# Row weighting of a graph attention layer: the order of its instructions written out over three blocks

## The chip, the core and the metric

The kernel runs on one core of a Trainium2 chip. Five engines of that core matter here, each with a queue of its own that runs in program order: TensorE (PE in the profile, with its weight loads as PEld), VectorE (DVE), ScalarE (ACT), GpSimd (POOL) and SyncE (SP), which only issues transfers. ACT, POOL and SP can all issue DMA transfers. The metric is the device time of one execution in microseconds, the median of several runs.

## What is computed

The reference takes 4096 node rows of 256 numbers and a 0/1 adjacency of 4096 x 4096, and runs two layers on them. The change touches the beginning of layer 0, a graph attention layer with 4 heads of 64:

```
h = relu(layernorm(x))
hW = (h @ W).reshape(n, 4, 64)
src = hW . a[:64];  dst = hW . a[64:]
e = leaky_relu(src[:, None] + dst[None, :], 0.2), masked by adj > 0
out = softmax(e) @ hW                 # per head
x = x + layernorm(out) * gamma + beta
```

Layer 1, a top-p diffusion over the same rows with two steps, takes most of the time and isn't changed.

## The kernel before, in words

The exponential of a leaky ReLU of a sum falls apart into products: where src + dst is positive the weight is exp(src) exp(dst), else exp(0.2 src) exp(0.2 dst). So the kernel first weights the rows: for each block b of 128 rows (32 blocks) it makes hW, multiplies each head's 64 columns by exp(dst) and by exp(0.2 dst), and appends the two factors as a 65th column. These 2 x 4 x 65 = 520 numbers (`uv`) are split into three bf16 parts, so that the later bf16 matmuls keep fp32's precision. That is the **row weighting** (lines 193 to 240). Then follow 16 **passes** (4 groups of 1024 destination rows by 4 heads). A pass walks over 16 pairs of blocks; for each pair it makes a sign matrix g (is src + dst positive?, 2 chunks of 128x1024), two masks m from g and the adjacency `ax` (lines 305 and 306), and 32 matmuls of the masks with the weighted rows `ut` (line 325).

The row weighting of one block, with its engine and line:

- DVE: statistics of the row (lines 153, 154); for each group of four blocks, POOL makes scale and bias in four small steps (lines 145 to 148).
- ACT: `hb`, the normalized row with ReLU (213). PE: two transpositions (216). ACT: the copy `hT` (218). PE: two matmuls with `wx`, the weights with eight more columns for src and dst (221). An fp32 matmul shows as two records.
- DVE: `sd_c`, src and dst of the block (222). ACT: two small exponentials (226). DVE: two products (228), which read PSUM.
- ACT: the first part, a cast (232). DVE: the first subtraction (233). ACT: the second part (237). DVE: the second subtraction, which is the third part (238).
- POOL: the copy of head 0's parts to `ut0` in SBUF (239). ACT's queue: the store of the other heads' parts to `uv_d` in DRAM (240). POOL: a small memset of the ones column (231).
- After blocks 3 and 7 (`b % 4 == 3`, below 8): four transpositions that spread src over 1024 columns into `sr0` for the first pass (245, 246). After every sixth block POOL issues a load of adjacency, `ax`, 512 KB (line 179, called at 236), so five of the eight loads start in this stage.

Before the loop, `wx` gets its eight columns by four products and sums on DVE (199, 201). After it come the transposition of src for all heads and its store `s_d` (248 to 251), the merged key weights `wkq` for layer 1 (254 to 263), d_big and d_neg (264, 265), which the signs need, and the factors `e_c` (268, 269), which the first pass needs at its end.

Buffers: three `uv` and four `st` slots (`split_rows`, `b % 4`). In this stage the program gives the operations block after block, and the framework's scheduler chooses the order in each engine's queue. The passes are different: there `manual_schedule` keeps the order in which the code calls the stages, `sign_stage(n + 3)`, `mask_stage(n + 2)`, `products(n)`, for ACT, DVE, PE and POOL. SP's order stays with the scheduler. Before the first products the signs of pairs 0 to 2 (ACT, line 299; pairs 3 and 11 of a pass are compared on DVE, line 297) and the masks of pairs 0 and 1 are made. `mask_stage` also issues, on SP, the loads of the next pass's source row `sr` (line 282, from s_d) and of its quarters `ut` (287, from uv_d), and the store of ut0's quarters (413).

Of the kernel before, what the change touches and what calls it, by code (L numbers as in the profile page):

```python
# [17 lines left out]
U8 = mybir.dt.uint8  # L18
# [38 lines left out]
def gat_then_top_p_diffusion(  # L57
# [53 lines left out]
    ln_g_r = row_vector(ln_g, "ln_g_r")  # L111
    ln_b_r = row_vector(ln_b, "ln_b_r")


    wkq = const.tile([P, KC, 2 * DA], F32, name="wkq")
    nc.scalar.dma_start(wkq[:, :, :DA], w3_t.rearrange("(k p) m -> p k m", p=P))
# [49 lines left out]
    with tc.tile_pool(name="l0", bufs=1) as l0, tc.tile_pool(name="l0s", bufs=2) as l0s, tc.tile_pool(name="l0o", bufs=1) as l0o:  # L166
        passing = ctx.enter_context(ExitStack())
        l0a, l0u = (passing.enter_context(tc.tile_pool(name=x, bufs=n)) for x, n in (("l0a", 9), ("l0u", 6)))
        gamma_r = row_vector(gamma, "gamma_r", l0)
        beta_r = row_vector(beta, "beta_r", l0)  # L170
# [17 lines left out]
        ut0 = [quarter() for q in range(4)]  # L188
        split_rows = l0o.tile([P, 4, 2 * H * (W3 + 1) // 2], F32, name="st")
        sr0 = l0s.tile([P, G0 * P], F32, name="sr")  # L190
        with tc.tile_pool(name="l0r", bufs=3) as rows, tc.tile_pool(name="l0w", bufs=1) as l0w, \
                tc.tile_pool(name="ps2", bufs=2, space=PSUM) as ps2:
            a_r = row_vector(a, "a_r", l0w)
            wx = l0w.tile([P, KC, D + 2 * H], F32, name="wx")
            nc.sync.dma_start(wx[:, :, :D], w.rearrange("(k p) m -> p k m", p=P))
            for k in range(KC):
                for i in range(2):
                    pr = rp.tile([P, H, HD], F32, name="pr", tag="hl", bufs=5)
                    nc.vector.tensor_mul(pr, wx[:, k, :D].rearrange("p (h d) -> p h d", h=H),
                                         a_r[:, None, ts(i, HD)].to_broadcast([P, H, HD]))  # L200
                    nc.vector.reduce_sum(wx[:, k, ds(D + i * H, H)], pr, axis=AX.X)
            for g in range(NB // 4):
                nc.sync.dma_start(X[:, ts(g, 4), :], x[ts(g, 4 * P), :].rearrange("(b p) d -> p b d", p=P))
            for g in range(NB // 4):
                x4 = X[:, ts(g, 4), :]
                mv = rows.tile([P, 4, nc.vector.BN_AGGR_DIM], F32, name="mv4")
                for i in range(4):
                    moments_of(mv[:, i, :], x4[:, i, :])
                rs, nmr = steps(mv, 4, rows)
                for i in range(4):  # L210
                    b = 4 * g + i
                    hb = rows.tile([P, D], F32, name="hb")
                    nc.scalar.activation(hb, x4[:, i, :], AF.Relu, scale=rs[:, i:i + 1], bias=nmr[:, i:i + 1])
                    pt = ps2.tile([P, KC, P], F32, name="tp")
                    for k in range(KC):
                        nc.tensor.transpose(pt[:, k, :], hb[:, ts(k, P)], ident)
                    hT = rp.tile([P, KC, P], F32, name="hT", tag="ar", bufs=4)
                    nc.scalar.copy(hT, pt)
                    pm = ps2.tile([P, 512], F32, name="mm", bufs=3)
                    for k in range(KC):  # L220
                        nc.tensor.matmul(pm[:, :D + 2 * H], hT[:, k, :], wx[:, k, :], start=(k == 0), stop=(k == KC - 1))
                    nc.vector.tensor_scalar(sd_c[:, :, :, b], pm[:, ds(D, 2 * H)].rearrange("p (t h) -> p t h", t=2),
                                            TINY, -TINY, ALU.add, ALU.add)
                    uv = rows.tile([P, H, 2, W1], F32, name="uv")
                    for t, scale in enumerate((1.0, ALPHA)):
                        nc.scalar.activation(uv[:, :, t, HD:], pm[:, ds(D + H, H)][:, :, None], AF.Exp, scale=scale)
                    for t in range(2):
                        nc.vector.tensor_mul(uv[:, :, t, :HD], pm[:, :D].rearrange("p (h d) -> p h d", h=H),
                                             uv[:, :, t, HD:].to_broadcast([P, H, HD]))
                    parts = split_rows[:, b % 4, :].bitcast(BF16).rearrange("p (h t w) -> p h t w", h=H, t=2)  # L230
                    set1 = nc.gpsimd.memset(parts[:, :, :, W3:], 1.0)
                    nc.scalar.copy(parts[:, :, :, :W1], uv)
                    nc.vector.tensor_tensor(uv, uv, parts[:, :, :, :W1], ALU.subtract)
                    if b % 6 == 5:
                        with tc.issue_after(set1.ins):
                            ax.append(edges(0, len(ax)))
                    nc.scalar.copy(parts[:, :, :, ds(W1, W1)], uv)
                    nc.vector.tensor_tensor(parts[:, :, :, ds(2 * W1, W1)], uv, parts[:, :, :, ds(W1, W1)], ALU.subtract)
                    nc.gpsimd.tensor_copy(ut0[b // QUARTER][:, b % QUARTER], parts[:, 0])
                    nc.scalar.dma_start(uv_d[1:, :, b].rearrange("h p t w -> p h t w"), parts[:, 1:])  # L240
                    if b % 4 == 3 and b < G0:
# [1055 lines left out]
```

## Time and profile before

| | us |
|---|---|
| median of 3 runs | 2957.44 (2957.43 to 2959.31) |
| the profiled execution | 2960.24 |
| its span, first to last instruction | 2958.3 |
| row weighting: block 0's exponential to block 31's | 22.75 to 120.80 |
| first product of the first pass | 131.3, without a gap from 131.98 |
| mean granted TensorE clock over the span | 0.987 |

Mean duration and count in the stage, from the groups of the first 155 us:

| line, engine | what | count | mean ns |
|---|---|---|---|
| 213 ACT | hb | 32 | 606 |
| 218 ACT | hT | 32 | 374 |
| 232, 237 ACT | casts 128x520 | 32 each | 636, 626 |
| 226 ACT | exponentials | 64 | 171 |
| 228 DVE | products 128x256 | 64 | 415 |
| 233, 238 DVE | subtractions 128x520 | 32 each | 724, 699 |
| 153, 154 DVE | statistics | 32 each | 400, 168 |
| 221 PE | matmuls | 128 | 518 |
| 239 POOL | copy to ut0, 128x392 bf16 | 32 | 708 |
| 146 POOL | power, one of four steps | 8 | 1102 |
| 179 POOL | adjacency issue | 8 | 840 |

How to read it: durations of neighbours on one engine overlap by about 0.1 us, so what a queue can carry is better read from start to start. An instruction that waited for a semaphore shows it as idle time before it, with the releaser; one that was held up while running shows a longer duration. Times of one engine are summed over the stage, and a full stage shows an engine near its length.

### The profile page before, as it was taken

How to read it: one execution, taken by the hardware profiler on the slowest of the kernel's cores; microseconds unless marked ns; L12 is line 12 of the kernel's file. 1: busy time of each engine (PE TensorE's matmuls, PEld its weight loads, DVE VectorE, ACT ScalarE, POOL GpSimd, SP SyncE). 2: the span in 40 equal slices, each digit the busy share in tenths (PEclk: the TensorE clock that was granted, in tenths of full speed). 3: DMA queues.
4: the chain of work that ended last, by engine and by line, in shares of the span. 5: the costliest groups of instructions: out<-in, count | busy, mean ns of one | idle time of the engine just before them, and what ended most of it. 6: DMA issues, size and time to landing. Idle time of an engine off the chain costs nothing. (4 is left out here: it accounts for less than half of the span.)

```text
span 2958.3 us, 51979 instructions
## 1 busy us (share of the span) xinstructions
PE 2829.7 (96%) x19033; PEld 2473.5 (84%) x19033; DVE 2196.5 (74%) x5195; ACT 1915.5 (65%) x3067; POOL 726.4 (25%) x1637
## 2 busy tenths in 40 slices
PE   4699999999999999999999999899999999999998
PEld 3499999999987778888888888788778888888886
DVE  6666877868754383788888888453837999999995
ACT  5768687867833544777777777234427777777772
POOL 3201111112010030322223322000203444444441
PEclk8799999999999999999999999999999999999999
DMA  6858668595454686000000000388980000001000
GB/s 154 176 208 238 187 223 194 223 235 169 191 192 156 219 277 214 19 20 20 20 20 26 20 20 18 131 272 271 330 289 22 25 25 25 25 27 31 25 23 21
DMA packets 181152, 368.16 MB, mean 124 GB/s; under 512 B 17168, under 2 KB 133904, under 8 KB 176784
## 3 DMA queue, kind: packets, MB, share of 16 engines
q1 hardware_dynamic: 129824, 261.55, 26.2%
q0 software_dynamic: 21504, 83.89, 11.9%
q10 hardware_dynamic: 29552, 19.22, 2.1%
q8 instruction: 155, 2.54, 0.3%
q14 instruction: 117, 0.96, 0.1%
HBM read 301.35 MB, written 109.38 MB: 139 GB/s over the span
## 5 line engine op out<-in xcount | busy, mean ns | idle before, releaser
L943 PE MATMUL acc<-X,eT 128*128 128x256 f32 x4096 | 968.1, 381 | 0.0
L943 PEld LDWEIGHTS acc<-X,eT 128*128 128x128 f32 x4096 | 744.8, 191 | 97.8 <-ACT eT L937 14.5
L325 PE MATMUL acc<-ut,m 128*128 128x195 bf16 (+1 forms) x8192 | 700.9, 247 | 13.9 <-DVE m L305 8.0
L325 PEld LDWEIGHTS <-m 128*128 128x128 fp8e4 x8192 | 696.6, 97 | 18.1 <-issue 9.9
L762 ACT ACTIVATE e<-mm,nm 128x1024 f32<-128x1024 f32 x256 | 286.7, 1120 | 311.6 <-PE mm L602 297.1
L299 ACT ACTIVATE g<-sr,d_big 128x1024 uint8<-128x1024 f32 x448 | 471.3, 1139 | 5.5 <-DMA s_d<-sT 2.9
L937 ACT COPY eT<-tp 128x512 f32<-128x512 f32 x512 | 299.2, 584 | 107.2 <-PE tp L935 106.3
L830 DVE SCALAR_TENSOR_TENSOR big<-e,c 128x4096 f32<-128x4096 f32 x58 | 273.0, 4707 | 121.2 <-POOL c L815 84.2
L502 PE MATMUL mm<-ar,hl 128*128 128x512 f32 x844 | 336.6, 402 | 13.1 <-DMA ar<-adj_d 5.4
L848 DVE MAX8 cand<-big 128x8 f32<-128x228 f32 (+1 forms) x1152 | 348.4, 380 | 0.0
L786 POOL TENSOR_TENSOR sums<-sums 128x2 f32<-128x2 f32 x64 | 12.5, 196 | 1313.0 <-ACT void L769 1313.0
L502 PE MATMUL acc<-ar,hl 128*128 128x512 f32 x844 | 329.4, 393 | 1.4 <-DVE ar L489 1.4
L935 PE MATMUL tp<-ident,e 128*128 128x128 f32 x2048 | 311.5, 275 | 7.8 <-DVEq L1234 5.8
L935 PEld LDWEIGHTS tp<-ident,e 128*128 128x128 f32 x2048 | 249.3, 141 | 77.2 <-ACT eT L957 27.8
L305 DVE TENSOR_TENSOR m<-g,ax 128x512 uint32<-128x512 uint32 x256 | 181.4, 709 | 127.6 <-PE acc L325 104.2
L872 DVE SCALAR_TENSOR_TENSOR e<-e,found 128x4096 f32<-128x4096 f32 x58 | 259.6, 4476 | 0.0
L769 ACT ACTIVATE void<-e,c1x 128x2048 int8<-128x2048 f32 x128 | 257.5, 2011 | 3.1 <-issue 2.2
L769 ACT ACTIVATE void<-e,c 128x2048 int8<-128x2048 f32 x128 | 257.4, 2011 | 0.0
L502 PEld LDWEIGHTS mm<-ar,hl 128*128 128x128 f32 x844 | 159.6, 189 | 52.0 <-issue 9.4
L602 PE MATMUL mm<-kT,qT 128*128 128x512 f32 x512 | 198.1, 468 | 3.6 <-ACT e L762 2.2
L306 DVE TENSOR_TENSOR m<-m,ax 128x512 uint32<-128x512 uint32 x256 | 177.1, 692 | 25.3
L502 PEld LDWEIGHTS acc<-ar,hl 128*128 128x128 f32 x844 | 159.6, 189 | 33.7 <-DVE ar L489 1.8
(262 smaller groups left out, 3444.2 us busy)
## 6 DMA issues: line engine op xcount, KB each, us to landing
ar<-adj_d SPq DMA_DIRECT2D x211, 512.0 KB, 4.6
adj_d<-ax POOLq DMA_DIRECT2D x32, 2048.0 KB, 7.0
ut<-uv_d SPq DMA_DIRECT2D x60, 784.0 KB, 5.2
aru<-adj_d SPq DMA_DIRECT2D x45, 512.0 KB, 4.5
ax<-in_adj_t_dram POOLq DMA_DIRECT2D x32, 512.0 KB, 15.7
x<-xf_d SPq DMA_DIRECT2D x78, 128.0 KB, 4.9
uv_d<-st ACTq DMA_DIRECT2D x32, 294.0 KB, 4.3
xf<-xft_d SPq DMA_DIRECT2D x64, 128.0 KB, 2.2
```

Source lines behind the costliest of these rows:

```text
L299: nc.scalar.activation(g[:, c, :], shared[k].sr, AF.Relu, scale=BIG, bias=d_big[:, h, j:j + 1])
L325: nc.tensor.matmul(shared[k].acc[i][:, t, :cols], m[t][:, c, ts(i, P)], shared[k].ut[j // QUARTER][:, j % QUARTER, t, :cols], start=(j == ...
L502: nc.tensor.matmul(A.acc[c][s], A.hl[m][:, t, ts(s, P)], A.ar[m][:, ts(c, 512)], start=(j == 0 and t == 0), stop=(j == NB - 1 and t == 1))
L602: nc.tensor.matmul(pm[:, h, :], q[t], kT[:, ds(h * (N // 2) + c * 512, 512)], start=(t == 0), stop=(t == 1))
L762: nc.scalar.activation(ev[:, :, c, :], r.pm[c], AF.Exp, bias=r.nm, accum_out=r.sums[:, c // 2, c % 2:c % 2 + 1])
L769: nc.scalar.activation(void, r.e[:, ts(h, N // 2)], (AF.Relu, AF.Sign)[i], bias=r.c1, scale=-1.0, accum_out=r.sums[:, h, 2 + i:3 + i])
L830: nc.vector.scalar_tensor_tensor(big, r.e, r.c3, r.e, ALU.is_le, ALU.mult, accum_out=r.low3)
L848: nc.vector.max(cand[:, s, :], big[:, edges[s]:edges[s + 1]])
L872: nc.vector.scalar_tensor_tensor(r.e, r.e, r.t, r.e, ALU.is_ge, ALU.mult, accum_out=kept)
L935: nc.tensor.transpose(pt[:, i, :], r.e[:, ts(4 * g + i, P)], ident)
L937: nc.scalar.copy(eT, pt)
L943: nc.tensor.matmul(r.acc[:, 0, :], eT[:, i, :], cur[:, j, :], start=(j == 0), stop=(j == NB - 1))
```

## The change

The row weighting is ordered by hand, as the passes are. The functions below are called once per block by `turn_of(b)`, which works on three blocks at once: block b is multiplied and read, block b - 1 weighed and its first part made, b - 2 gets its second part, b - 3 its third part, copy and store; block b + 1 is opened (hb and transpositions), and the statistics run six blocks ahead.

- **Loads.** The rows X are issued first on SP (group 0, then the vector a, then groups 1 to 7). wx and the small weights go by ACT's queue. gamma, beta, ln_g and ln_b come after the rows. SP's order is kept in this part.
- **Splits on GpSimd.** The second subtraction is halved: heads 0 and 1 on DVE, heads 2 and 3 on POOL. The store to uv_d is issued by SP. The memset of the ones is done once for each slot, at the start. d_big and d_neg are made on POOL, by quarters of eight blocks.
- **Buffers.** Eight slots: four of `st`, four in two free `ut` buffers. Five `uv`: three in the tile of output rows, one in the second `sr` buffer, one in an `ax` buffer. PSUM: the eight banks of the passes' accumulators serve the stage too (two for transpositions, three for products, others for spread and keys), and no pool is closed between.
- **Into the stage.** The signs of pairs 0 and 1 are made chunk by chunk on POOL in turns 14, 15, 19 and 20; the masks of these pairs in turns 30 and 31. The merged keys are made in turn 12. Six adjacency loads (blocks 1, 6, 11, 16, 21, 26) start in place of five.
- **Into the first pass.** `turn_of(32)` to `turn_of(34)`, that is the remaining splits of blocks 29 to 31, run after the products of pairs 1 to 3; the factors e_c after those of pairs 4 and 5.

The core of the diff:

```diff
-        with tc.tile_pool(name="l0r", bufs=3) as rows, tc.tile_pool(name="l0w", bufs=1) as l0w, \
-                tc.tile_pool(name="ps2", bufs=2, space=PSUM) as ps2:
...
-                    nc.scalar.copy(parts[:, :, :, :W1], uv)
-                    nc.vector.tensor_tensor(uv, uv, parts[:, :, :, :W1], ALU.subtract)
...
-                    nc.scalar.copy(parts[:, :, :, ds(W1, W1)], uv)
-                    nc.vector.tensor_tensor(parts[:, :, :, ds(2 * W1, W1)], uv, parts[:, :, :, ds(W1, W1)], ALU.subtract)
-                    nc.gpsimd.tensor_copy(ut0[b // QUARTER][:, b % QUARTER], parts[:, 0])
-                    nc.scalar.dma_start(uv_d[1:, :, b].rearrange("h p t w -> p h t w"), parts[:, 1:])
...
+            block_rows(0)
+            nc.scalar.dma_start(wx[:, :, :D], w.rearrange("(k p) m -> p k m", p=P))
+            nc.sync.dma_start(a_r, bass.AP(tensor=a.tensor, offset=a.offset, ap=[[0, P], [1, 2 * HD]]))
+            for g in range(1, NB // 4):
+                block_rows(g)
...
+            slots = [l0o.tile([P, 4, HALF], F32, name="st")] + [l0u.tile([P, 2, HALF], F32, name="slots", tag="ut") for i in range(2)]
...
+            def first_part(b):
+                nc.scalar.copy(slots[b % len(slots)][:, :, :, :W1], uvs[b % len(uvs)])
+
+            def second_part(b):
+                uv, parts = uvs[b % len(uvs)], slots[b % len(slots)]
+                nc.vector.tensor_tensor(uv, uv, parts[:, :, :, :W1], ALU.subtract)
+                nc.scalar.copy(parts[:, :, :, ds(W1, W1)], uv)
+
+            def third_part(b):
+                uv, parts = uvs[b % len(uvs)], slots[b % len(slots)]
+                for engine, h in ((nc.vector, slice(0, H // 2)), (nc.gpsimd, slice(H // 2, H))):
+                    engine.tensor_tensor(parts[:, h, :, ds(2 * W1, W1)], uv[:, h], parts[:, h, :, ds(W1, W1)], ALU.subtract)
+                seen = nc.gpsimd.tensor_copy(ut0[b // QUARTER][:, b % QUARTER], parts[:, 0])
+                nc.sync.dma_start(uv_d[1:, :, b].rearrange("h p t w -> p h t w"), parts[:, 1:])
+                if b % 5 == 1 and len(ax) < 6:
+                    with tc.issue_after(seen.ins):
+                        ax.append(edges(0, len(ax)))
...
+            def turn_of(b):
+
+                if b < NB:
+                    multiplied(b)
+                if 0 < b < NB:
+                    weighed(b - 1)
+                opened(b + 1)
+                if b % 4 == 0 and 0 < b <= G0:
+                    spread(b - 1)
+                if 0 < b <= NB:
+                    first_part(b - 1)
+                if 1 < b <= NB + 1:
+                    second_part(b - 2)
+                if 2 < b <= NB + 2:
+                    third_part(b - 3)
+                measured(b + 6)
+                if b < NB:
+                    read(b)
+                if b % QUARTER == 0 and 0 < b < NB:
+                    signed(b // QUARTER - 1)
+                if b == 12:
+                    merged_keys()
+                for n, at in enumerate((14, 19)):
+                    if at <= b < at + 2:
+                        sign_stage(n, b - at)
+                if NB - 2 <= b < NB:
+                    mask_stage(b - NB + 2)
...
-            for n in range(3):
-                sign_stage(n)
-            mask_stage(0)
-            mask_stage(1)
...
+        rest = {n: lambda b=NB - 1 + n: turn_of(b) for n in (1, 2, 3)}
+        rest.update({4 + i: lambda i=i: factors(i) for i in range(2)})
+        with tc.manual_schedule(engines=every):
+            for b in range(4):
+                measured(b)
...
+            opened(0)
+            for b in range(NB):
+                turn_of(b)
+            weighed(NB - 1)
...
+            signed(3)
+            sign_stage(2)
             for n, (k, p) in enumerate(todo):
                 if n > 0 and p == 0:
                     later.extend(evacuate(k - 1))
                 sign_stage(n + 3)
                 mask_stage(n + 2)
                 products(k, p, ms.pop(n))
+                if n in rest:
+                    rest[n]()
```

## The prediction

> **What bounds the kernel now.** I read the page's shares first, then stretches of the start by engine, then waits and groups of the first 155 us, and at last the timeline from 0 to 170 us, row by row. The shares of the span:
> ```profile
> PE 2829.7 (96%) x19033; PEld 2473.5 (84%) x19033; DVE 2196.5 (74%) x5195; ACT 1915.5 (65%) x3067; POOL 726.4 (25%) x1637
> ```
> TensorE is busy 96% of 2958.3 us, so only a place where it idles can give much. The stretches (from:to, length, busy us and instructions of PE, PEld, DVE, ACT, POOL, then granted clock, DMA share, GB/s) show the place:
> ```profile
> 20.00:40.00 20.00, 15.56 (x56) 10.85 (x54) 15.64 (x52) 13.81 (x42) 8.01 (x18) 0.91 0.39 86
> 53.27:60.28 7.01, 3.74 (x16) 2.22 (x14) 6.56 (x15) 4.86 (x15) 1.42 (x2) 1.00 1.04 102
> 80.00:100.00 20.00, 9.77 (x24) 5.57 (x23) 11.49 (x27) 10.93 (x30) 10.33 (x23) 0.59 0.60 153
> 120.00:131.30 11.30, 2.58 (x10) 1.37 (x8) 5.37 (x14) 6.86 (x15) 2.32 (x4) 0.50 0.99 163
> 131.30:175.00 43.70, 43.34 (x491) 42.88 (x492) 26.35 (x39) 32.70 (x33) 4.04 (x6) 0.96 0.74 163
> ```
> From 131.3 us TensorE is full, 43.34 of 43.70; before, in the row weighting, no engine is. From 80 to 100 us the fullest, DVE, has 11.49 of 20. So that stage is a chain of waits, and a microsecond taken from it shifts all that follows. Its waits (total us, times, longest):
> ```profile
> PEld mm L221 <- ACT hT L218: 38.5, 25, 4.9
> POOL st L231 <- DMA uv_d<-st: 32.2, 11, 8.9
> ...
> ACT hb L213 <- POOL nmr L148: 16.5, 1, 16.5
> ...
> ACT st L232 <- DMA uv_d<-st: 7.9, 4, 3.5
> ```
> The stores of the parts hold the chain: the four `st` slots are refilled only when the store of uv_d has landed (4.3 us in the middle, 11.4 at most). ACT, stopped there by program order, lets TensorE wait for `hT`. Three moments of the timeline (start, duration) divide the stage:
> ```profile
> 22.75 0.24 ACT L226 ACTIVATE uv<-mm 128x4 f32<-128x4 f32 x2 [1.16 <-DVE sd_c L222]
> ...
> 120.80 0.24 ACT L226 ACTIVATE uv<-mm 128x4 f32<-128x4 f32 x2 [0.35 <-DVE sd_c L222]
> ...
> 131.98 0.34 PE L325 MATMUL acc<-ut,m 128*128 128x196 bf16 x1 [0.36 <-DVE m L306]
> ```
> The first is block 0's exponential, the second block 31's, the third the point from which products run without a gap. So: head 22.75, middle 98.05 (31 steps of 3.16), tail 11.18.
>
> **Head.** The rows X leave first instead of at 6.15 us, behind five small loads and wx; wx goes by ACT's queue. Now a row load lands 7.0 to 9.6 us after its issue (8.6 in the middle), the first load of an empty SP queue after 3.7. Rows issued at 0.75 arrive between 0.75 + 3.7 + 1.5 (0.5 MB at the 350 GB/s of that time) = 6 and 0.75 + 8.6 = 9.4; I take 6, since the queue is empty. Then four blocks of statistics 1.6, the four GpSimd steps 1.9 (16.61 to 18.45), and from `hb` to the exponential 4.3 (18.49 to 22.75): 13.8, say 14, at worst 17.2. The wx branch is no later: 0.77 + its present 7.4, then 2.7 for the four products and sums (11.86 to 14.51), 10.9, while the first matmul comes near 12. **Gain 8.75.** The row vectors for the ends of both layers are moved behind the rows; nothing reads them for 100 us.
>
> **Middle.** Per block, from the groups:
> ```profile
> L239 POOL COPY ut<-st 128x392 bf16<-128x392 bf16 x32 | 22.5, 708 | 30.9 <-DVE st L238 30.9
> L238 DVE TENSOR_TENSOR st<-uv,st 128x520 bf16<-128x520 f32 x32 | 22.4, 699 | 2.7 <-ACT st L237 1.5 <-POOL ut L239 0.7
> ```
> ACT has hT, hb, two casts and two exponentials. Start to start in rows without a wait they take 0.26, 0.51, 0.53, 0.52 and 0.12, together 1.94; its store issue goes to SP's queue. DVE has the two products 0.67, the first subtraction 0.62, half the second 0.35, statistics 0.39, sd_c 0.1: 2.1. PE has 1.16 + 0.5 warm. The chain through a turn is exponentials 0.24, products 0.74, first cast 0.53, second 0.52 with its subtraction beside it, small hand-overs: 2.2. Five `uv` and eight slots in place of three and four let three blocks overlap; a slot is wanted again 5.5 turns after its store, 13 us, above the longest landing of 11.4. So the DMA waits go, and what is late next is this ACT/DVE chain. The present order already goes that fast where nothing stalls: 2.34 per block from 53.27 to 60.28, with the DMA at 1.04, and 2.19 for six blocks from 101.20 to 114.33. **I take 2.4**, bounds 2.19 and 2.7: 31 x 2.4 = 74.4 for 98.05, gain 23.7.
>
> GpSimd decides whether 2.4 holds. Its half of the second subtraction, 128x260, isn't in the trace; the nearest row on that engine:
> ```profile
> L376 POOL TENSOR_TENSOR X<-X,beta_r x32: 715/736/1019, 331.0 to 861.2; 128x256 f32<-128x256 f32 x32
> ```
> So 0.74, at most 1.02; below, 0.35 (DVE's rate for half). With the copy to `ut` 0.50 (1.06 at most), steps 0.48 (15.3 us for eight groups over 32 blocks) and adjacency issue 0.17, GpSimd has 1.9 per turn: it fits. It collides with DVE, though. At 56.12 a copy of 0.51 began on POOL, at 56.16 a subtraction on DVE, which took 1.02 and not 0.67. In the new order the GpSimd half runs beside DVE's products, which read PSUM and show no such stretch (407 to 421 ns), and the copy beside the statistics; hence little is lost. If nothing fits beside, DVE's 0.70 + 0.37 and GpSimd's 1.9 add to 2.96 per turn, my first rival. [...]
>
> **Put into the middle**: two `spread` copies, 1.1 of transposes or 0.6 of ACT each, 2.4 with hand-overs (they are in the 98.05 too); `merged_keys`, 2.0 by its rows at 121 to 123.9; one mask pair on DVE, 2 x 0.69 = 1.4 (the second lies behind the last exponential). Four sign chunks on GpSimd, 128x1024 each: no row. By the copy's rate (0.50 for 392) 1.3 each, by the subtraction's (0.74 for 256) 2.9; I take 1.5, since a compare reads one input as the copy does: 6 us, of which two turns of buffers hide all but 2.2. From below nothing, from above 8. [...] Sum 8.0, bounds 5 and 14.
>
> **Tail.** Now: last split to 125.3, s_d stored at 121.6, row read back at 128.28, signs, first mask at 130.5. After: signs and masks of pairs 0 and 1 lie in the middle, the last three blocks' rest beside the first products, which need only quarter 0. One transposition and its wait remain: 1.0 (0 to 2). Gain 10.2. What it adds to the first pass: ACT 1.6 for splits and 0.6 for factors against its slack, 28 signs of 1.04 in 43 us; DVE under 5 us. Two covers are thin. `uvs` takes the second `sr` buffer, so the source row of pass 1 waits for pass 0's last sign; today the next row is issued at 157.52, when TensorE is at pair 9.4 of 2.71 us, six pairs ahead. After, ACT ends near T+30 and the row lands 4.9 later, T+35, before pair 16 at T+43. Uncovered it costs up to 5 once. And uv_d's stores share SP's queue with reloads that wait for TensorE; they come earlier in the program.
>
> **Sum.** 14 + 74.4 + 8.0 + 1.0 = 97.4 for 131.98: 34.6 less. The profiled execution took 2960.24 (span 2958.3 and 1.9 around it), 2.8 above the median of the runs, 2957.44. So 2925.6 profiled, **2923** as median.
>
> **Rivals.**
> - *Turn about 2.95.* [...] 14 + 91.5 + 8 + 1 = 114.5, gain 17.5: 2940. A DMA that can't keep up ends here too: its share adds to 95 us by 131.3, and a sixth adjacency load (34 us for five) adds 6.8; but the stores need only 31 of it.
> - *Given back in the first pass.* The pass-1 row, a reload or an adjacency block comes late, TensorE idles 5 to 25: 2940 with the middle as forecast, 2950 with both.
> - *Slower.* GpSimd becomes the bound of every turn. It decides from (131.98 - 14 - 8 - 1) / 31 = 3.52 per turn, that is from 2.36 for the half subtraction in place of 0.74. With bf16 operands at three times the row, 2.2, the copy always blocked at 1.06, steps 0.7, issue 0.17 and signs at 2.9 (0.4 per turn), it is 4.5: 14 + 140 + 8 + 1 = 163, 31 later: 2988. Against it: no two-input row of 256 on POOL exceeds 1.02.
> - *It doesn't do what it says.* Landings grow with eight stores in flight and the slots still wait: the turn stays at 3.16, gain 11: 2946.
>
> **How the numbers follow.** Likeliest, turn 2.19 to 2.7: 0.62, from 12.5 + 67.9 + 5 + 1 = 86.4 (2912) to 17.2 + 83.7 + 10 + 2 = 112.9 (2938). Turn 2.95: 0.17. Given back: 0.06. Slots still wait: 0.04. Slower: 0.09. No change, by parts of these that cancel: 0.02. The range reaches below to ACT's own 1.94 per block (12.5 + 60.1 + 5 + 1 = 78.6, 2904; I stop at 2907) and above to the slots' 2946: 2907 to 2946. Faster by over 0.2% (5.9 us, about what a measurement of this kernel can tell): 0.62 + 0.17 + 0.06 + 0.04 = 0.89, less 0.01 for the ends; within 0.03; slower 0.09.
>
> **What would show it.** In the new profile: block 0's exponential near 14; exponentials 2.4 apart; no wait of ACT or POOL for uv_d; a clock near 1.0 from 20 to 95; the half subtraction on POOL near 0.74; the first products without a gap near 97, and no gap at pair 16, some 43 us later; the rest of the page the same. It is wrong if POOL has the longest busy time of the stage, if L213's successor waits for POOL's steps, or if TensorE idles after its first product.

## The result, and the profile after

| | before | after |
| --- | --- | --- |
| median of the runs, us | 2958.38 (2957.43 to 2960.55, 4 runs) | 2938.49 (2936.8 to 2939.0, 4 runs) |
| profiled execution, us | 2960.24, span 2958.3 | 2939.0, span 2937.2 |
| block 0's exponential | 22.75 | 14.46 |
| block 31's exponential | 120.80 | 114.63 |
| first product without a gap | 131.98 | 114.81 |
| head, middle, tail | 22.75, 98.05, 11.18 | 14.46, 100.17, 0.18 |

The ratio of the times is 0.9931, with a 95% interval from 0.9914 to 0.9948: 19.9 us faster, where 34.6 were forecast. The whole kernel after the change still has TensorE as its bound, as the first part of its page shows:

```profile
PE 2832.3 (96%) x19033; PEld 2476.5 (84%) x19033; DVE 2197.3 (75%) x5193; ACT 1912.0 (65%) x3063; POOL 761.9 (26%) x1657
```

Against before POOL's sum has grown by 35.5 us, PE's and PEld's by 3.0 at most. The three moments of the timeline after (start, duration, engine and line) divide the stage as before; L249 is the exponential now, L378 the product:

```profile
14.46 0.24 ACT L249 ACTIVATE o<-b 128x4 f32<-128x4 f32 x2 [1.92 <-DVE sd_c L246]
...
114.63 0.23 ACT L249 ACTIVATE o<-b 128x4 f32<-128x4 f32 x2
114.81 10.43 PE L378 MATMUL acc<-ut,m 128*128 128x196 bf16 x104
```

The head came 8.3 earlier and the tail is gone: the products start 0.18 after the last exponential, 11 less than before. The middle, which was to shrink from 98 to 82.4, is 2.1 **longer** than before. So the time to look for is 17.8 us (100.17 - 82.4), all of it between 14 and 115 us. The stretches of after (from:to, length, then busy us and instructions of PE, PEld, DVE, ACT, POOL, then granted clock, DMA share, GB/s):

```profile
40.00:60.00 20.00, 14.77 (x40) 10.06 (x41) 14.22 (x40) 14.39 (x41) 11.52 (x21) 0.57 0.69 142
60.00:80.00 20.00, 13.16 (x38) 8.35 (x37) 15.76 (x44) 13.29 (x37) 19.33 (x22) 0.66 0.65 137
80.00:100.00 20.00, 12.99 (x34) 7.97 (x33) 14.20 (x38) 11.87 (x34) 18.05 (x23) 0.57 0.77 130
...
111.00:155.00 44.00, 41.62 (x461) 40.86 (x462) 33.73 (x55) 35.59 (x43) 12.01 (x16) 0.96 0.91 212
```

Two things stand out: the granted clock is near 0.6 from 40 to 100 us, and POOL is full from 60 to 100 us (19.33 and 18.05 of 20). From 111 on TensorE is full, beside the remainders too. The waits from 0 to 115 us (total us, times, longest) name no store of uv_d any more. Another wait has grown, that of the exponential for sd_c. Before, from 0 to 132 us, it was

```profile
ACT uv L226 <- DVE sd_c L222: 7.7, 10, 1.3
```

and after it is 13.9 in 21 times, by the tile that is written:

```profile
PEld b L242 <- ACT hT L239: 39.5, 32, 2.5
...
ACT hb L232 <- POOL nmr L143: 14.6, 3, 8.3
...
ACT o L249 <- DVE sd_c L246: 10.8, 15, 1.9
...
ACT sr L249 <- DVE sd_c L246: 1.7, 3, 0.9
...
ACT uv L249 <- DVE sd_c L246: 1.4, 3, 0.6
```

The distance from one block's exponential to the next (31 of them) has its median at 3.0 us, not 2.4. Five are long: 3.95 and 5.62 (the two `spread` turns), 5.12 (the keys), 4.14 and 6.25 (the signs), together 25.1. The other 26 take 75.1, that is 2.89 each. So, counted in this way, 15.1 of the 17.8 are 31 turns of 2.89 in place of 2.4, and 2.7 are what the put-in work cost above its 8.0 (100.17 - 31 x 2.89 = 10.7). After the first product the profiled executions differ by up to 8 us (from it to the end of the span 2820 to 2828 us over before, after and the kernels below, with 2826.3 before and 2822.4 after; nothing in that part of the program differs among most of them). Nearly all of this lies in layer 1: the 16 passes take 704.7 to 707.2 in all these traces, the rest 2114 to 2122, in the main the longer the lower the granted clock there (0.997 where it is 2114.3, in e7; 0.992 where it is 2122.2, in e1). For causes in the row weighting the first product's time is therefore the cleaner measure; differences between medians below some 4 us are not read. The first product has a scatter of its own, which the end of the experiments measures.

### The profile page after: what moved, and what is told of

Its sections match the earlier page's. It is cut to its first block, busy times and chain, and to the rows that moved or that the text cites. A ratio compares the mean times of both kernels' runs of the same rounds, so it can differ in the third digit from the quotient of the medians.

```text
span 2937.2 us, 51997 instructions
## 1 busy us (share of the span) xinstructions
PE 2832.3 (96%) x19033; PEld 2476.5 (84%) x19033; DVE 2197.3 (75%) x5193; ACT 1912.0 (65%) x3063; POOL 761.9 (26%) x1657
## 5 line engine op out<-in xcount | busy, mean ns | idle before, releaser
L378 PE MATMUL acc<-ut,m 128*128 128x195 bf16 (+1 forms) x8192 | 700.5, 247 | 5.5 <-DVE st L395 5.5
L378 PEld LDWEIGHTS <-m 128*128 128x128 fp8e4 x8192 | 696.7, 97 | 9.4 <-DVE st L395 4.6
```

The source lines that it names most:

```text
L378: nc.tensor.matmul(shared[k].acc[i][:, t, :cols], m[t][:, c, ts(i, P)], shared[k].ut[j // QUARTER][:, j % QUARTER, t, :cols], start=(j == ...
```

## What ends a turn

Three theories were tried, and the change's parts were undone one by one.

- **A, cold TensorE** ("cold" is half clock, a granted clock of 0.50 in the turn at 32.06 of after, where a block's four matmuls take 2.13; "warm" is full clock, 1.00 from 53.27 to 60.28 of before, where they take 1.16). Cold, the loop matmuls, sd_c, exponential, hT, matmuls gives 3.0. The clock is the cause, and a filled TensorE cures it.
- **S, signs.** The four compares on GpSimd hold up its steps (mean and scale of later groups) and DVE.
- **C, the order at the PSUM bank.** Found on the way, in the second experiment. sd_c (DVE, L246) and the exponential (ACT, L249) both read the products' bank, and the framework orders these two readers as the program has them: the exponential waits for sd_c, 13.9 in after. sd_c stands at the end of DVE's turn, so the loop is exponential, products, subtraction, half subtraction, statistics, sd_c, exponential, on one engine and back, at any clock.

A cold turn in the timeline of after:

```profile
32.06 0.24 ACT L249 ACTIVATE o<-b 128x4 f32<-128x4 f32 x2 [0.62 <-DVE sd_c L246]
...
32.21 0.37 ACT L239 COPY hT<-b 128x256 f32<-128x256 f32 x1
32.40 0.76 DVE L254 TENSOR_TENSOR o<-b,o 128x256 f32<-128x256 f32 x2 [0.44 <-ACT o L249]
...
32.64 2.13 PE L242 MATMUL b<-wx,hT 128*128 128x264 f32 x4 [0.46 <-ACT hT L239]
33.07 0.69 DVE L262 TENSOR_TENSOR o<-o,slots 128x520 f32<-128x520 f32 x1
...
34.80 0.17 DVE L246 TENSOR_SCALAR sd_c<-b 128x8 f32<-128x8 f32 x1
35.01 0.24 ACT L249 ACTIVATE o<-b 128x4 f32<-128x4 f32 x2 [0.58 <-DVE sd_c L246]
```

Here the matmuls take 2.13 and end when sd_c can start; hT comes behind the exponential in ACT's program order, and the next matmuls behind hT. From 32.06 to 35.01 it is 2.95, and this goes round. GpSimd's work end to end with DVE's, the ground of the rival "turn about 2.95", is not what makes this turn: L262 has its 0.69 here. Over the stage DVE's subtractions are stretched in some turns. Of the 30 subtractions L262 from 18 to 114 us 22 took 0.68 to 0.69, and the eight longer ones add 2.8; of the half subtractions on DVE all but five took 0.42 or 0.43, and these five (0.73 to 0.89, most beside POOL's own half) add 2.2. That is 5 us in all, 0.16 per turn.

## The experiments

Each kernel is the changed one with the edit shown; five rounds each, against the kernel before on the same chip (that had 2953.9 to 2960.5 from chip to chip, so gains are compared, not times).

**e1: the signs on DVE.**

```diff
                 if len(only) == 1:
-                    nc.gpsimd.tensor_scalar(g[:, c, :], shared[k].sr, d_neg[:, h, j:j + 1], 255.0, ALU.is_gt, ALU.mult)
+                    nc.vector.tensor_scalar(g[:, c, :], shared[k].sr, d_neg[:, h, j:j + 1], 255.0, ALU.is_gt, ALU.mult)
```

> The four early sign chunks (pairs 0 and 1) are compared on DVE and not on GpSimd. Theory A (TensorE at the half clock sets the turn of 3.0 us, and GpSimd's compares of 3.7 us add delays in turns 15 to 23): the delays above 3.0 in turns 15, 16, 19, 22 and 23 (0.4 + 0.2 + 1.1 + 0.3 + 3.3 = 5.4 us) go, the four compares on DVE cost 0.75 each of which some shows, the other turns stay near 3.0; first product at 109 to 111 instead of 114.8, about 2933 us. [...] If the compares are hidden: 2938 to 2941.

Measured: 0.9934 [0.9921, 0.9947], gain 17.9; first product 108.6, 6.2 earlier than after's. Most turns are 2.7 to 3.0 as before, the two long sign turns are gone (none above 3.41 from turn 13 on). S holds, but not for all of the 6.2: 2.0 of them lie in turns 1 to 14, before the first sign, where the two programs are the same, and some 4.3 in turns 15 to 31. The median doesn't show them. Its cause in the trace of after is the duration itself:

```profile
L348 POOL TENSOR_SCALAR g<-sr,d_neg 128x1024 uint8<-128x1024 f32 x4 | 15.2, 3796 | 0.2
```

and what it delays, in the timeline of after:

```profile
61.31 3.72 POOL L348 TENSOR_SCALAR g<-sr,d_neg 128x1024 uint8<-128x1024 f32 x1
61.55 1.42 DVE L262 TENSOR_TENSOR sr<-sr,slots 128x520 f32<-128x520 f32 x1
```

```profile
83.99 3.70 POOL L348 TENSOR_SCALAR g<-sr,d_neg 128x1024 uint8<-128x1024 f32 x1
...
91.16 0.20 POOL L143 TENSOR_TENSOR nmr<-nmr,rs 128x4 f32<-128x4 f32 x1
91.39 0.60 ACT L232 ACTIVATE hb<-X,nmr,rs 128x256 f32<-128x256 f32 x1 [4.20 <-POOL nmr L143]
```

Signs of 3.7 put back POOL's steps for later blocks, and `hb` waits 4.20 for them. The DVE subtraction that starts 0.24 after the first sign takes 1.42 in place of 0.69 (more on this in the last section).

**e2: TensorE kept busy.** Two bf16 matmuls of 128x512 per turn, into a free bank; their result is not used.

```diff
                 opened(b + 1)
+                if b < NB:
+                    fill = in_bank(2, [P, 512])
+                    ones_ = ident.bitcast(BF16)
+                    for i in range(2):
+                        nc.tensor.matmul(fill.rearrange("p (a b) -> p a b", a=2), ones_[:, :P], ones_[:, None, :].to_broadcast([P, 2, 2 * P]), start=True, stop=True)
```

> Two matmuls without use (bf16, 128x128 by 128x512, into a PSUM bank that nothing reads) after the transpositions of each turn; all else as in the changed kernel. Theory A: they fill TensorE's wait for hT, its clock stays near 1.0, the four matmuls of a block take 1.16 and not 2.13, and the turns of 3.0 become 2.3 to 2.5; some 20 turns by 0.6 is 12 us: first product near 103, about 2926. [...] If the added work only delays TensorE: up to 0.9 us per cold turn more, 2955.

Measured: 0.9946 [0.9933, 0.996], gain 16.3; first product 112.4. The clock over the middle rises from 0.71 to 0.91 (below, the whole middle of after, then of e2), yet the middle falls by 2.6 only:

```profile
14.46:114.63 100.17, 66.21 (x200) 43.52 (x200) 74.26 (x205) 68.19 (x190) 71.78 (x104) 0.71 0.75 150
```

```profile
14.70:112.30 97.60, 64.58 (x264) 39.62 (x263) 72.87 (x205) 67.68 (x189) 73.24 (x104) 0.91 0.76 153
```

Warm turns are 2.75, not 2.3 to 2.5. So A by itself falls. What ends them stands in the timeline of e2:

```profile
54.11 0.24 ACT L249 ACTIVATE sr<-b 128x4 f32<-128x4 f32 x2
...
54.66 1.16 PE L242 MATMUL b<-wx,hT 128*128 128x264 f32 x4 [0.21 <-ACT hT L239]
...
55.12 0.69 DVE L262 TENSOR_TENSOR o<-o,slots 128x520 f32<-128x520 f32 x1
...
56.63 0.14 DVE L246 TENSOR_SCALAR sd_c<-b 128x8 f32<-128x8 f32 x1
56.86 0.24 ACT L249 ACTIVATE uv<-b 128x4 f32<-128x4 f32 x2 [0.39 <-DVE sd_c L246]
```

The matmuls are done at 55.82, but sd_c comes at 56.63, when DVE has got through its subtractions and statistics; the exponential waits for it. This is C.

**e3: the bank read a turn later**, so that sd_c and the exponential stand at the start of DVE's and ACT's turn. **e4** is e3 with e1.

```diff
                 if 0 < b < NB:
+                    read(b - 1)
                     weighed(b - 1)
...
                 measured(b + 6)
-                if b < NB:
-                    read(b)
```

> The exponentials and sd_c of block b are issued one turn later, behind the copy hT of block b + 1, so that TensorE's next matmuls no longer wait for ACT's exponential of the block before. Nothing else is changed. Theory A: the loop matmul, sd_c, exponential, hT, matmul is cut; TensorE either warms, turn 2.3 to 2.5, or is full at the half clock, 2.76: first product 14.5 + 31 x (2.3 to 2.8) + 11 + 2 = 99 to 114, about 2922 to 2937, likely 2928. [...]

> Signs of pairs 0 and 1 on DVE, and exponentials one turn later, both edits together. Theory A: the gains add, 5 and 10 us: about 2923. [...]

Measured: e3 0.9966 [0.9953, 0.9979], gain 9.7, first product 117.3, slower than after; e4 0.9946 [0.9932, 0.9959], gain 15.0, first product 111.4, later than e1's 108.6. The cold turn of 3.01 stays, with another loop. In the timeline of e3:

```profile
44.32 2.12 PE L242 MATMUL b<-wx,hT 128*128 128x264 f32 x4 [0.46 <-ACT hT L239]
...
46.24 0.63 PE L235 MATMUL b<-ident,hb 128*128 128x128 f32 x2
...
46.91 0.37 ACT L239 COPY hT<-b 128x256 f32<-128x256 f32 x1
...
47.33 2.12 PE L242 MATMUL b<-wx,hT 128*128 128x264 f32 x4 [0.46 <-ACT hT L239]
```

Matmuls 2.12, transpositions 0.63, the copy hT 0.37: the transpositions of the next block stand behind the matmuls on TensorE, and at half clock this alone is 3.01. So at half clock more than one loop has this length here, and the edit, which takes only one of them away, gains nothing in such a turn.

**e5: the exponential first.** In the program the exponentials now stand before sd_c, so sd_c waits for them and not the other way round.

```diff
-                nc.vector.tensor_scalar(sd_c[:, :, :, b], pm[:, ds(D, 2 * H)].rearrange("p (t h) -> p t h", t=2),
-                                        TINY, -TINY, ALU.add, ALU.add)
                 for t, scale in enumerate((1.0, ALPHA)):
                     nc.scalar.activation(uv[:, :, t, HD:], pm[:, ds(D + H, H)][:, :, None], AF.Exp, scale=scale)
+                nc.vector.tensor_scalar(sd_c[:, :, :, b], pm[:, ds(D, 2 * H)].rearrange("p (t h) -> p t h", t=2),
+                                        TINY, -TINY, ALU.add, ALU.add)
```

> In read(b) the two exponentials are given before sd_c, not after it; nothing else differs from the changed kernel. Theory C (a loop through two engines sets the turn: exponential on ACT, products, subtraction, half subtraction, statistics and sd_c on DVE, then the next exponential, which is made to wait for sd_c because both read one PSUM bank): the exponential now waits for the matmuls alone, so the warm turn falls from 2.75 to about 2.35 and the cold one from 3.01 to about 2.8 (matmuls 2.13, exponential, hT); some 25 turns by 0.2 to 0.4 is 5 to 10 us: first product at 105 to 110, 6 to 10 us less than the changed kernel. Theory A alone (half clock): the cold loop loses only sd_c's 0.2 per turn, 3 to 4 us. [...]

**e6** is e5 with e1's signs on DVE, **e7** is e6 with e2's filler.

> Exponentials before sd_c, and the early sign chunks on DVE in place of GpSimd. Theory C: the gains of both add, first product at 100 to 105, 10 to 15 us less than the changed kernel; DVE has room for four compares of 0.75. [...]

> Exponentials before sd_c, early signs on DVE, and besides two matmuls without use per turn after the transpositions. If both loops, C's and the half clock's, set the time: warm turns of 2.3, first product at 14.5 + 31 x 2.35 + 9 = 96 to 99, some 16 us less than the changed kernel. If the clock doesn't matter any more once C's loop is cut: as without the filler, within 2 us.

| | ratio | gain | first product | middle | its clock |
| --- | --- | --- | --- | --- | --- |
| after | 0.9931 [0.9914, 0.9948] | 19.9 | 114.8 | 100.2 | 0.71 |
| e5 | 0.9928 [0.9915, 0.9942] | 20.7 | 110.7 | 95.6 | 0.77 |
| e6 | 0.9905 [0.989, 0.9921] | 28.3 | 102.6 | 87.4 | 0.82 |
| e7 | 0.9891 [0.9876, 0.9907] | 33.3 | 102.4 | 87.2 | 0.98 |

A warm turn in the timeline of e5 (L247 is the exponential, L248 sd_c):

```profile
28.30 0.23 ACT L247 ACTIVATE o<-b 128x4 f32<-128x4 f32 x2
...
28.56 0.17 DVE L248 TENSOR_SCALAR sd_c<-b 128x8 f32<-128x8 f32 x1
...
28.84 1.16 PE L242 MATMUL b<-wx,hT 128*128 128x264 f32 x4 [0.89 <-ACT hT L239]
...
30.56 0.23 ACT L247 ACTIVATE o<-b 128x4 f32<-128x4 f32 x2
```

The wait for sd_c is gone and the turn is 2.26, where after had 2.62 to 2.75 with statistics in a warm turn. In its place sd_c now waits for the exponential (9.7, 8.2 and 6.0 us by tile, from 0 to 111 us): the order of the program decides which of the two waits. C holds: the edit takes 4.1 from the first product by itself and 6.0 together with e1's (e6 against e1). The cold turns of 3.0 remain in e5 and fewer of them in e6. What the clock is worth beyond that, e7 answers only as a net: the filler brings it from 0.82 to 0.98 and the first product by 0.2, but the filler costs time too (the two `spread` turns are 4.36 in e7 and 3.93 in e6). The turns themselves show both causes. Taken are turns 1 to 25 without the `spread` turns and the keys; a turn is cold when its four matmuls take over 1.9, warm when they take under 1.3:

| | cold turns, median | warm turns, median |
| --- | --- | --- |
| old order: after | 14, 3.00 | 5, 2.75 |
| old order, filler: e2 | 2, 2.97 | 17, 2.75 |
| exponential first: e5 | 12, 3.02 | 7, 2.27 |
| exponential first, signs on DVE, filler: e7 | none | 19, 2.34 |

A cold turn is 3.0 in either order, a warm one 2.75 in the old order. Only with both cured is it near 2.3. The median of e7 is 5 us better than that of e6, but their intervals overlap and the difference would have to lie after the first product, where the two kernels do the same. Their traces differ by 7.4 there, with the granted clock of layer 1 at 0.993 and 0.997.

**e8: the half subtraction back on DVE**, whole.

```diff
-                for engine, h in ((nc.vector, slice(0, H // 2)), (nc.gpsimd, slice(H // 2, H))):
+                for engine, h in ((nc.vector, slice(0, H)),):
```

> One part of the change undone: the whole second subtraction on DVE, none on GpSimd. Theory C: DVE's loop takes 0.3 more, the turn becomes 3.0 to 3.1 warm and cold, GpSimd's collisions go; 3 to 8 us more than the changed kernel. [...]

Measured: 0.9928 [0.9914, 0.9941], gain 20.4; first product 112.2, 2.6 **earlier** than after's, which is within the scatter of one trace. Plain turns are 2.89 to 2.96, and 2.36 where no statistics are left. GpSimd's share of the splits brings nothing that shows in this kernel.

**e9: four slots** in place of eight.

```diff
+            slots = slots[:4]
             for t in slots:
```

> One part of the change undone: four slots in place of eight (the two further buffers stay allotted, unused). If the waits for the stores were a real bound that the eight slots removed: a slot is wanted 1.5 turns, 4.5 us, after its store, landings are 4 to 11 us, so ACT waits for uv_d again in a third of the blocks; first product at 120 to 130 instead of 114.8, 5 to 15 us more than the changed kernel. If the loop through DVE and the half clock would have held the turn anyway: within 3 us.

Measured: 0.9967 [0.9957, 0.9976], gain 9.0; first product 125.2, 10.4 later than after's. The waits for the stores return, in the list of waits of e9 from 0 to 130 us:

```profile
ACT st L259 <- DMA uv_d<-st: 19.6, 7, 4.8
```

The slots do what the forecast said: without them the stores hold ACT again.

**e10: the tail undone.** Signs and masks of pairs 0 and 1, and the remainders, stand before the passes again.

```diff
-                for n, at in enumerate((14, 19)):
-                    if at <= b < at + 2:
-                        sign_stage(n, b - at)
-                if NB - 2 <= b < NB:
-                    mask_stage(b - NB + 2)
...
-            sign_stage(2)
+            for n in sorted(rest):
+                rest.pop(n)()
+            for n in range(3):
+                sign_stage(n)
+            mask_stage(0)
+            mask_stage(1)
```

> One part undone: no early signs and masks, and the last three blocks' remainders and the factors before the passes; the first product then waits for them, as before the change. Theory of the text (the tail's 11 us are gained, some 6 of them paid back by the compares on GpSimd): block 31's exponential comes 6 to 9 us earlier than in the changed kernel, at 106 to 109, the first product 10 to 13 us after it, at 117 to 121: 3 to 6 us more than the changed kernel. Rival (the compares were hidden, the tail's gain is net): first product at 124 to 126, 10 us more.

Measured: 0.9947 [0.9933, 0.9961], gain 18.6; the first product without a gap at 114.67, within 0.2 of after's 114.81, so both expectations missed. TensorE in the timeline of e10 (L497 is the transposition at the end of the weighting):

```profile
105.01 0.33 PE L497 MATMUL b<-ident,sd_c 128*128 128x128 f32 x1 [0.47 <-DVE sd_c L246]
113.94 0.34 PE L373 MATMUL acc<-ut,m 128*128 128x196 bf16 x1 [8.60 <-DVE m L353]
114.67 11.56 PE L373 MATMUL acc<-ut,m 128*128 128x196 bf16 x110 [0.38 <-DVE m L354]
```

The tail is back, 9.6 from the last exponential (105.10), and the middle is 9.7 shorter (90.5 for 100.2). But 3.9 of the 9.7 lie in turns 1 to 14, where the programs are the same. From turn 15 on, where the moved signs and masks stand, it is 5.8. So moving this work cost the middle some 5.8 of the 9.4 that the tail gave back, and that both kernels start their products at the same time is chance as to the other 3.9. The medians (18.6 and 19.9) can't tell. With the signs on DVE (e1) the last exponential is at 108.5 and nothing behind it, 6 earlier than either.

**e11: the rows late.** The four row vectors, a and wx go first on SP again, then all rows.

```diff
-            block_rows(0)
-            nc.scalar.dma_start(wx[:, :, :D], w.rearrange("(k p) m -> p k m", p=P))
+            ln_g_r, ln_b_r = row_vector(ln_g, "ln_g_r"), row_vector(ln_b, "ln_b_r")
+            gamma_r, beta_r = row_vector(gamma, "gamma_r", l0), row_vector(beta, "beta_r", l0)
             nc.sync.dma_start(a_r, bass.AP(tensor=a.tensor, offset=a.offset, ap=[[0, P], [1, 2 * HD]]))
-            for g in range(1, NB // 4):
+            nc.sync.dma_start(wx[:, :, :D], w.rearrange("(k p) m -> p k m", p=P))
+            for g in range(NB // 4):
                 block_rows(g)
```

> One part undone: the loads in the old order, row vectors first, then a and wx, then the rows, all on SP's queue. If the order of the loads made the head shorter: block 0's exponential at 20 to 23 instead of 14.5, and all that follows shifts by it, 6 to 8 us more than the changed kernel. If the head was set by the order of DVE's work (sums for wx before the statistics) instead: 14.5 to 17, under 3 us.

Measured: 0.9967 [0.9956, 0.9977], gain 10.3; block 0's exponential at 21.43, 7.0 later than after's, the first product at 119.05, 4.2 later. In the timeline of e11:

```profile
21.43 0.24 ACT L248 ACTIVATE o<-b 128x4 f32<-128x4 f32 x2 [1.92 <-DVE sd_c L245]
```

The order of the loads makes the head. The middle is 2.6 shorter than after's, all of it in turns 1 to 14: scatter.

**e12: all that helped**, as a kernel of its own: e7, with the copy of each `spread` one turn after its transpositions, and the merged keys made before block 0 while the rows are on their way. Its edits beyond those shown:

```diff
-                nc.scalar.copy(sr0[:, ds((b - 3) * P, 4 * P)], pm)
+                pro.wide = pm
...
                     spread(b - 1)
+                if b % 4 == 1 and 1 < b <= G0 + 1:
+                    nc.scalar.copy(sr0[:, ds((b - 5) * P, 4 * P)], pro.wide)
...
-                if b == 12:
-                    merged_keys()
...
                 measured(b)
+            merged_keys()
             opened(0)
```

> A version meant to beat both: exponentials before sd_c, early signs on DVE, matmuls without use in each turn, the merged keys made before block 0, and the copy of the spread source row one turn after its transpositions, so that ACT doesn't wait for them. Against the version without the last two edits, turns 4 and 8 fall from 4.36 to about 3, turn 13 from 3.4 to 2.3: first product at 98 to 99, 3 to 4 us less. If ACT is held by something else there: as that version, first product at 102.

Measured: 2925.23, 0.9882 [0.9864, 0.9899], gain 34.3; first product 98.1. It is faster than both kernels; against e7 (33.3) the median doesn't tell, the first product is 4.3 earlier. The middle of e12:

```profile
14.50:97.50 83.00, 60.18 (x258) 37.19 (x256) 75.79 (x208) 65.00 (x187) 59.35 (x100) 0.98 0.92 180
```

83.0 at a clock of 0.98, with DVE at 75.8 of it and the DMA at 0.92: these two have little room left. The two spread turns are 2.27 and 2.70 (4.36 each in e7). Seven of its turns are 3.34 to 4.06 (four of them the signs on DVE, one the mask, and two in which `hb` waits 1.30 for POOL's steps), together 25.1; the other 24 take 57.9, which is 2.41 each.

**What one trace can tell.** The first sign starts after block 14's exponential. Up to there after, e1 and e10 run the same program, and so does e11 but for the order of the loads. Their times and clocks up to it, and from it to block 31's exponential:

| | after | e11 | e1 | e10 | e2 | e5 | e6 | e7 |
| --- | --- | --- | --- | --- | --- | --- | --- | --- |
| turns 1 to 14 | 46.1 | 43.3 | 44.1 | 42.2 | 42.1 | 41.6 | 38.7 | 39.8 |
| clock in them | 0.70 | 0.77 | 0.81 | 0.81 | 0.96 | 0.80 | 0.91 | 0.96 |
| turns 15 to 31 | 54.1 | 54.3 | 49.8 | 48.3 | 55.5 | 54.0 | 48.7 | 47.4 |

So the same program differs by up to 3.9 us from trace to trace, and after has the slowest of the four. Two turns make most of it, the second `spread` turn (5.63 in after, 3.94 in the other three) and the keys (5.13 for 3.23 in e1 and e10), and in the keys' turn the granted clock differs with it, 0.50 in after, then 1.00 in e1:

```profile
52.66:57.78 5.12, 4.09 (x13) 2.65 (x11) 2.40 (x7) 2.84 (x9) 2.94 (x7) 0.50 0.89 291
```

```profile
52.55:55.78 3.23, 2.03 (x10) 1.48 (x10) 2.39 (x7) 2.69 (x9) 1.44 (x4) 1.00 1.04 370
```

The gains of single edits given above carry this scatter; those of e2 and e8 at the first product are smaller than it, that of e5 (4.1) is about as large. For C the warm turns speak, and that e5 (only just) and e6 are below all four in turns 1 to 14; for S the second stretch speaks, where after and e11 agree within 0.2 and e1 and e10 are 4 to 6 below them.

## Why the prediction was right and where it was wrong

- **Direction, and what bounds the stage: right; the size was a rival's.** The median of 2938.5 lies between 2907 and 2946, but 15.5 above the 2923 that was added up. It is where a rival with a chance of 0.17 had put it. The start was a chain of waits, TensorE is full behind it, and what the first product came earlier (17.2) is what the time fell by (19.9), within the scatter named above.
- **Head, gain 8.75: right.** 8.3 measured; with the loads in the old order (e11) 7.0 of it are lost.
- **Stores, eight slots and five `uv`: right.** No wait for uv_d is left; four slots cost 10.4 (e9), and bring 19.6 of ACT's waits back.
- **Half subtraction on POOL, 0.74: right in size** (0.65 to 0.68 in most turns, up to 1.16 in the others). That it was needed for the turn was not: without it the first product is no later (e8: 2.6 earlier, within the scatter).
- **"The chain through a turn ... 2.2", "I take 2.4": here it failed.** Turns of 2.89 in place of 2.4 make 15.1 of the 17.8. The chain was drawn through the values alone: exponentials, products, casts. It left out the readers of the products' bank, of which the exponential stood second, behind sd_c and so behind DVE's whole turn. The wait was in the lines of the prediction itself (the exponential idle before sd_c, 1.16 and 0.35) and was not followed: in the old order sd_c came early on DVE, in the new one last. Once it is turned round (e5), a warm turn is 2.27 in place of 2.75, and in e12 the plain turn is 2.41. The order alone is not the whole of it: a cold turn stays at 3.0 with it (e5), so the clock has its part too. What each is worth of the 15.1 is not taken apart; the order took 4.6 from the middle by itself (e5) and 6.5 with the signs on DVE (e1 to e6). So the sums of the engines' shares, 2.1 for DVE and 1.94 for ACT, were no worse than needed; the dependence between them was missing.
- **The rival "turn about 2.95": right in the figure.** Plain turns 2.89, first product 114.8 (114.5 given), median 2938.5 (2940 given). Its 2.96 put all of GpSimd's work end to end with DVE's; no run shows that, and the stretched rows are worth 0.16 per turn. A cold TensorE is what most turns show: 14 of the 22 turns that the experiments sort are cold, with a median of 3.0, near that figure. Before had such turns too: its four matmuls take 2.13 each time at 64.73 and 67.75, 3.02 apart, at a granted clock of 0.50. But the cold TensorE is not the only bound: warm (e2) the turn is still 2.75, for which the prediction had no rival. Warmed alone it gains 2.4 at the first product, and warmed after C and S are cured (e7 against e6) 0.2, both net of the filler. Why TensorE goes cold is not shown; in e5 and e6 it did so out of warm turns of 2.27 as well (turn 10).
- **"a clock near 1.0 from 20 to 95": wrong.** It was 0.63 there. The forecast took 2.4 with a warm TensorE from the stretch of 2.34 per block in before, where the clock was 1.00. A warm stretch shows that a turn can be short at a full clock, not that the clock stays full. In the cold turn at 32 us TensorE is busy for 2.49 of 2.95 us (84%), at a granted clock of 0.50:

```profile
32.06:35.01 2.95, 2.49 (x7) 1.62 (x6) 2.39 (x7) 2.21 (x7) 1.64 (x4) 0.50 1.07 211
```

In turns 10 to 12, at 81%, it is 0.50 as well (last section). What lowers it, no run here shows.
- **Four signs on GpSimd, 1.5 each: mis-sized.** 3.7 to 4.1 each, 15.2 together, above the upper bound of 2.9 too. The bounds were two kinds of operation, a copy and a subtraction, taken per element; a compare with two operations and a bytes' output was neither. "All but 2.2" was to be hidden: on DVE instead they cost some 4.3 less in turns 15 to 31 (e1), and `hb` waited 4.20 for POOL's steps, one of the signs of being wrong that the prediction had named.
- **The tail, gain 10.2: right on its face, less than half as a net.** 11.0 came off the tail against before; of the 9.4 that e10 gives back, the work put into the middle cost some 5.8. The put-in sum of 8.0 had one mask pair and the signs at 3.6; measured by e10 they are 5.8.
- **First pass: right.** No gap at pair 16, and the remainders don't stretch it: from the first product without a gap to the start of the last, over all 16 passes, it is 705.8 us in both.

From after to e12 the middle falls by 17.2, in the order of the steps that were run: signs to DVE 6.3, exponential first 6.5, filler 0.2, keys and spread 4.2, each with the scatter of single traces. That e12 ends at 83.0, near the 82.4 of the forecast, is in part by chance: the forecast had keys and spread copies in the middle (4.4), e12 doesn't, and its signs on DVE cost more than 2.2.

Left open: what lowers the clock of layer 1 in some executions; how the 15.1 divide between order and clock; and what lowers the clock in the row weighting. None of it was tried for itself.

## What to carry to other kernels

When work is put in order by hand, draw each engine's turn with its position: a short instruction at the end of a long turn (sd_c, 0.14 to 0.17 us of its own) is as late as the whole turn, and the exponential, which reads the same PSUM bank after it in the program, waited for it (13.9 in after). Put the reader that others need first. A piece moved off the path is gained only if the engine that takes it has room at that place: undo it alone to see the net, and compare the two traces stretch by stretch, so that a difference from before the edit acts isn't counted for it. Price an operation on GpSimd by a row of the same operation, not by rows of others: the sign, put at 1.5 from a copy and a subtraction, took 3.7 to 4.1.

## What the runs showed of the hardware

- A compare with a multiply on GpSimd, 128x1024 from f32 to bytes, took 3.70 to 4.08 us in after; in the same stage the copy of 392 took mostly 0.51 and the half subtraction of 260 mostly 0.66.
- A DVE subtraction took longer beside some GpSimd instructions of after than beside others. In four places DVE's half subtraction, 0.42 alone, took 0.88 to 0.89: it overlapped POOL's own half by 0.60 and was some 0.46 longer. POOL's half, 0.66 alone, took 1.03 to 1.16 there. Beside the compare, the two that began 0.24 and 0.37 after it (1.42 and 1.28) both ended 1.65 to 1.66 after its start, as if they had run their 0.69 from 0.96 on; six that began later in a compare and ended before it kept their 0.69 or 0.42. The third compare, which began while a DVE subtraction was running, with the half subtraction right behind it, is the one of 4.08; these two kept their 0.69 and 0.42, so there the compare is the longer one.
- TensorE stayed at half clock, 0.50, through turns 10 to 12 of after, in which it was busy for 7.54 of 9.27 us, 81% of the time:

```profile
43.39:52.66 9.27, 7.54 (x19) 5.14 (x20) 7.67 (x21) 6.67 (x19) 7.04 (x12) 0.50 0.99 146
```

- Two more bf16 matmuls of 512 columns per turn brought the granted clock of the middle from 0.71 (after) to 0.91 (e2), and from 0.82 (e6) to 0.98 (e7) with the shorter turn.
- Early in the trace of after the granted clock and the matmuls don't agree: it reads 1.00 from 14.46 to 18.00, while the block's four matmuls at 15.10 take 2.13, as they do at 32.64, where it reads 0.50. So the 0.71 over its middle is a little high, and the length of a matmul tells more.
